# State sums of a selective scan: transposing accumulation replaced by identity matmuls with h as the moving operand, backward direction in reversed time

## The chip, the cores and the metric

The kernel runs on one core of a Trainium2 chip. The metric is the device time of one execution in microseconds (us), as the median of several runs. A profile is of one profiled execution; its span runs from the first to the last instruction of the program. The engines are TensorE (PE in the profile; PEld is its weight load, which can run beside a matmul), VectorE (DVE), ScalarE (ACT), GpSimd (POOL) and SyncE (SP), whose queue issues the DMAs.

## The reference

Four layers work on x of shape (16, 256, 256): an adapter of low rank, a bidirectional selective state-space layer with an MLP, and two attention blocks with MLPs. All is float32. The change lies in the state-space layer. For each of the two directions it computes this, the backward one on a flipped sequence whose result is flipped back:

```
def _ssm(h, in_w, xproj_w, dt_bias, A_log, Dskip, out_w):
    xz = h @ in_w
    xs, z = jnp.split(xz, 2, axis=-1)
    xs = jax.nn.silu(xs)
    proj = xs @ xproj_w
    dt = jax.nn.softplus(proj[..., :D_INNER] + dt_bias)
    Bm = proj[..., D_INNER:D_INNER + D_STATE]
    Cm = proj[..., D_INNER + D_STATE:]
    A = -jnp.exp(A_log)
    def step(hst, ins):
        dt_t, B_t, C_t, x_t = ins
        dA = jnp.exp(dt_t[:, :, None] * A)
        hst = hst * dA + (dt_t * x_t)[:, :, None] * B_t[:, None, :]
        y_t = jnp.einsum('bds,bs->bd', hst, C_t)
        return (hst, y_t)
    ...
    y = jnp.swapaxes(ys, 0, 1) + xs * Dskip
    return y * jax.nn.silu(z) @ out_w
...
h_fwd = _ssm(h, fwd_...)
h_bwd = jnp.flip(_ssm(jnp.flip(h, 1), bwd_...), 1)
x = x + gate * (h_fwd + h_bwd)
```

There are 512 inner channels, 64 states and 256 positions for each of 16 sequences in the batch.

## The kernel before

**Units and steps.** A unit is one sequence b in one direction d (0 forward, 1 backward), so there are 32 units. Each unit is worked off state by state: step k = (u, s) handles state s of unit u, for all 512 channels and 256 positions at once. There are 2048 steps. A tile of a step holds 128 partitions (channels within a block) x 4 blocks x 256 positions.

**One step.** `drive` (L931, POOL) makes h = dt·x·B for the state; the B rows come from DRAM, spread over the partitions by a DMA. `decay` (L946, ACT) makes exp(dt·A) into one of three PSUM tiles, two channel blocks at a time. `scan` (L974, DVE) runs the recurrence over time in place in h, in two instructions of 128x512. Then h is multiplied by the state's C row: in five of eight steps on DVE (L977), with the row spread over the partitions by two transposes on TensorE (`spread`, L961) into a double-buffered PSUM tile `cs`; in the other three steps on POOL (L981), with the row fetched by a DMA. `add_up` (L992, PE) adds h to the unit's sum `y` in PSUM. It does so by eight 128x128 transposes with accumulation: a block of h is the stationary operand, the identity is the moving one, and `y` has time on the partitions and channels along the free dimension. In the first step of a unit the skip term x·D is added in the same way.

**Backward units.** Their tensors stand in forward time. `decay` reads dt through a reversed view (`when`), takes the channel blocks in reversed order, and the scan works on a reversed view of h.

**End of a unit.** Two steps after the last scan of a unit, the sum leaves PSUM: ACT copies it (`yt`, L1165), eight transposes bring it back to channels on the partitions (`py`, L1172), and DVE multiplies it by the gate silu(z) out of PSUM (`yg`, L1173, two of 128x512). `back` then applies the output weights (`po`, L473) and adds the result to x (L480).

**Beside the scan** run the preparation of a later unit (`front`: input and dt projections, copies at L398, Silu, B and C rows) and the remaining layers of the previous sequence (`rest`: MLP, two attentions, two more MLPs), cut into small pieces by generators. One piece of `front` and one or two of `rest` are taken per step.

**What sets the order.** The kernel is written in Tile: the source gives dependencies and a program order in which `drive` is 4 steps ahead of the scan (`AHEAD`) and `add_up` 2 steps behind (`BEHIND`). A planner with its own instruction costs then fixes one order for each engine at build time, and each engine runs its list strictly in that order. The products on POOL are pinned to the program order. A step's h is one of eleven tiles (`NH`), which the skip term shares; `y` is a single PSUM tile of two banks, the three decays take three banks, `cs` one, and the work beside has two.

Of the kernel before, what the change touches and what calls it, by code (L numbers as in the profile page):

```python
# [15 lines left out]
P = 128  # L16
# [38 lines left out]
def kernel(ctx: ExitStack, tc: tile.TileContext, a: dict, out: bass.AP):  # L55
# [317 lines left out]
    def front(u):  # L373
# [15 lines left out]
        for m in range(0, 2 * IC, 2):  # L389
            px = halves(bank1("pxz"))  # L390
            for j in range(2):
                for c in range(DC):
                    nc.tensor.matmul(  # L393
                        px[:, j], w_in[:, c, (m + j) * P : (m + j + 1) * P], hT[:, c],
                        start=(c == 0), stop=(c == DC - 1),
                    )
                yield
            nc.scalar.copy(xz[:, m : m + 2], px)  # L398
        nc.scalar.activation(xz, xz, AF.Silu)
        exp_table()  # L400
        yield
# [63 lines left out]
    def back(u, yg):  # L465
# [12 lines left out]
        for m in range(DC):  # L478
            xb = xs[b][:, m]
            nc.vector.scalar_tensor_tensor(  # L480
                xb, po[:, m], m_mamba[:, 4 + m, b : b + 1], xb, ALU.mult, ALU.add
            )
        if d == 1:
            waiting.append(rest(b))
# [450 lines left out]
    def decay(k):  # L935
        u, s = steps[k]
        d = units[u][1]

        when = slice(1, T) if d == 0 else slice(T - 2, None, -1)
        made[k] = []  # L940
        for i in range(2):
            dc = decays[turn[0] % ND]
            turn[0] += 1
            for j in range(2):
                c = 2 * i + (j if d == 0 else 1 - j)
                nc.scalar.activation(  # L946
                    dc[:, j, 1:T], st[u][3][:, c, when], AF.Exp, scale=a_neg[d][:, c, s : s + 1]
                )
            made[k].append(dc)

# [13 lines left out]

    def scan(k):
        u, s = steps[k]
        d = units[u][1]
        h = hs[k]
        for i, dc in enumerate(made.pop(k)):
            hv = h[:, 2 * i : 2 * i + 2].rearrange("p c t -> p (c t)")  # L970
            dv = dc.rearrange("p c t -> p (c t)")
            if d == 1:
                hv = hv[:, ::-1]
            nc.vector.tensor_tensor_scan(hv, dv, hv, 0.0, ALU.mult, ALU.add)  # L974
        if k in nth:
            c = cs[:, nth[k] % 2]
# [7 lines left out]
    def add_up(k):  # L984
        u, s = steps[k]
        if s == 0:
            ys[u] = ps_y.tile([P, NT, DI], F32, name="y")

        for n, h in enumerate(([skips.pop(u)] if s == 0 else []) + [hs.pop(k)]):
            for t in range(NT):  # L990
                for c in range(IC):
                    nc.tensor.matmul(  # L992
                        ys[u][:, t, c * P : (c + 1) * P], h[:, c, t * P : (t + 1) * P], ident,
                        start=(s == 0 and n == 0 and c == 0),
                        stop=(s == NS - 1 and c == IC - 1), is_transpose=True,
                        skip_group_check=True,
                    )

# [144 lines left out]
    for k in range(len(steps) + BEHIND):  # L1145
# [13 lines left out]
        if k >= BEHIND:  # L1159
            u, s = steps[k - BEHIND]  # L1160
            if s == NS - 1:
                b, d = units[u]
                yt = s1.tile([P, NT, DI], F32, name="yt", tag="uu")
                for t in range(NT):
                    nc.scalar.copy(yt[:, t], ys[u][:, t])  # L1165
                yg = s1.tile([P, IC, T], F32, name="yg", tag="pr")
                for i in range(2):
                    py = halves(bank1("py"))
                    for j in range(2):
                        c = 2 * i + j  # L1170
                        for t in range(NT):
                            nc.tensor.transpose(py[:, j, t * P : (t + 1) * P], yt[:, t, c * P : (c + 1) * P], ident)  # L1172
                    nc.vector.tensor_tensor(  # L1173
                        yg[:, 2 * i : 2 * i + 2], py, st[u][0][:, IC + 2 * i : IC + 2 * i + 2], ALU.mult
                    )
                pend = beside((u, yg), u + 2)
        step(pend)
        for _ in range(2 if k % 2 else 1):
# [36 lines left out]
```

## Time and profile before

| | us |
|---|---|
| median of 3 runs | 7622.63 (7620.03 to 7626.16) |
| span of the profiled execution | 7616.3 |
| DVE busy | 6860.6 |
| POOL busy | 6843.8 |
| PE busy | 6249.2 |
| ACT busy | 5431.2 |
| sums over the states (L992), PE busy | 2385.3 |

The profiled execution's own time is not listed apart from its span; the median lies 6.3 us above the span. Busy time of an engine is the time covered by its instructions. A matmul's record includes the time in which it passes through the array, so records that follow closely overlap: their mean duration is longer than the pace at which they follow each other, and the pace is read from the length of an unbroken run. In a group's line the part after the bar gives the busy time, the mean in ns, and the idle time of the engine just before these instructions, with what ended most of it. In a table by stretch each engine has its busy time and, in brackets, its number of instructions.

### The profile page before, as it was taken

How to read it: one execution, taken by the hardware profiler on the slowest of the kernel's cores; microseconds unless marked ns; L12 is line 12 of the kernel's file. 1: busy time of each engine (PE TensorE's matmuls, PEld its weight loads, DVE VectorE, ACT ScalarE, POOL GpSimd, SP SyncE). 2: the span in 40 equal slices, each digit the busy share in tenths (PEclk: the TensorE clock that was granted, in tenths of full speed). 3: DMA queues.
4: the chain of work that ended last, by engine and by line, in shares of the span. 5: the costliest groups of instructions: out<-in, count | busy, mean ns of one | idle time of the engine just before them, and what ended most of it. 6: DMA issues, size and time to landing. Idle time of an engine off the chain costs nothing.

```text
span 7616.3 us, 100847 instructions
## 1 busy us (share of the span) xinstructions
PE 6249.2 (82%) x35471; PEld 4952.4 (65%) x35471; DVE 6860.6 (90%) x6887; ACT 5431.2 (71%) x12141; POOL 6843.8 (90%) x2959
## 2 busy tenths in 40 slices
PE   7568888888888888888888888888888888888778
PEld 4456676666667666676666666666666766666655
DVE  3988999999999999999999999999999999999982
ACT  4567777777777777777777777777777777777753
POOL 3999999999999999999999999999999999999960
PEclk8679999999999999999999999999999999999999
DMA  4112232222322222232222223222232222322221
GB/s 166 54 65 92 89 102 76 87 92 88 103 85 93 80 91 95 92 103 73 88 92 91 100 86 98 78 92 93 87 106 79 94 84 89 101 91 89 73 68 49
DMA packets 331644, 675.90 MB, mean 89 GB/s; under 512 B 24724, under 2 KB 204032, under 8 KB 326784
## 3 DMA queue, kind: packets, MB, share of 16 engines
q1 hardware_dynamic: 331136, 669.44, 26.7%
q8 instruction: 280, 4.59, 0.2%
q14 instruction: 228, 1.87, 0.1%
HBM read 650.22 MB, written 10.75 MB: 87 GB/s over the span
## 4 chain that ended last, share of the span: by engine, by line
DVE 47%; POOL 15%; issue 14%; ACT 12%; PE 10%; DVEq 0%; POOLq 0%; ACTq 0%
DVE h L974 34%; POOL h L931 8%; DVE h L977 8%; ACT decay L946 5%; POOL h L981 5%; PE y L992 3%; DVE maxima L682 1%; ACT L155 1%; PE dense L500 1%; PE down L511 1%; PE bank L108 1%; PE po L605 1%; POOL uu L452 1%; POOL dt L458 1%; POOL dtx L461 1%
## 5 line engine op out<-in xcount | busy, mean ns | idle before, releaser
L974 DVE TENSOR_TENSOR_SCAN h<-decay,h 128x512 f32<-128x512 f32 x4096 | 4748.8, 1213 | 283.1 <-ACT decay L946 196.6
L931 POOL TENSOR_TENSOR h<-dtx,bb 128x1024 f32<-128x1024 f32 x2048 | 4793.5, 2367 | 129.2 <-PE y L992 128.4
L992 PE MATMUL y<-ident,h 128*128 128x128 f32 x16384 | 2385.3, 292 | 693.0 <-POOL h L981 639.1
L992 PEld LDWEIGHTS y<-ident,h 128*128 128x128 f32 x16384 | 2054.6, 151 | 1047.6 <-POOL h L981 733.1
L946 ACT ACTIVATE decay<-dt,a_neg_bwd 128x255 f32<-128x255 f32 x4096 | 1816.8, 471 | 759.9 <-DVE h L974 718.3
L946 ACT ACTIVATE decay<-dt,a_neg_fwd 128x255 f32<-128x255 f32 x4096 | 1824.6, 474 | 613.0 <-DVE h L974 571.6
L981 POOL TENSOR_TENSOR h<-h,cb 128x1024 f32<-128x1024 f32 x768 | 1813.2, 2361 | 289.8 <-DVE h L974 275.1
L977 DVE TENSOR_TENSOR h<-h,cs 128x1024 f32<-128x1024 f32 x1280 | 1533.5, 1215 | 66.2 <-PE cs L961 56.6
L961 PE MATMUL cs<-ident,cT 128*128 128x128 f32 x2560 | 521.6, 294 | 131.8 <-DVE h L977 130.3
L961 PEld LDWEIGHTS cs<-ident,cT 128*128 128x128 f32 x2560 | 331.4, 147 | 216.0 <-DVE h L977 192.0
L572 PE MATMUL sc<-k,q 64*128 64x256 f32 x960 | 293.4, 429 | 16.7 <-ACT ex L581 16.0
L393 PE MATMUL pxz<-hTm,w_in 128*128 128x256 f32 x1024 | 267.6, 388 | 15.9 <-DVE maxima L682 12.1
L679 PE MATMUL sc<-kd,qk 128*128 128x512 f32 x490 | 251.4, 614 | 33.5 <-DVE maxima L682 20.8
L700 PE MATMUL scT<-qk,kd 128*128 128x256 f32 x984 | 251.1, 386 | 28.7 <-DVE qk L691 23.2
L581 ACT ACTIVATE ex<-sc,nmax 128x256 f32<-128x256 f32 x480 | 222.7, 468 | 71.2 <-DVE nmax L577 68.5
L423 PE MATMUL pdt<-xz,w_dt 128*128 128x256 f32 x1024 | 247.3, 385 | 0.0
L572 PEld LDWEIGHTS sc<-k,q 64*128 64x128 f32 x960 | 172.6, 200 | 105.3 <-issue 34.2
L393 PEld LDWEIGHTS pxz<-hTm,w_in 128*128 128x128 f32 x1024 | 181.4, 194 | 53.1 <-DVE maxima L682 15.5
L700 PEld LDWEIGHTS scT<-qk,kd 128*128 128x128 f32 x984 | 175.5, 190 | 60.7 <-ACT pr L429 25.0
L577 DVE TENSOR_REDUCE nmax<-sc 128x2 f32<-128x512 f32 x240 | 163.9, 683 | 49.5 <-PE sc L572 48.8
L423 PEld LDWEIGHTS pdt<-xz,w_dt 128*128 128x128 f32 x1024 | 190.7, 194 | 22.2
L595 ACT COPY exT<-pt 128x512 f32<-128x512 f32 x240 | 140.0, 583 | 86.2 <-PE pt L591 84.0
(350 smaller groups left out, 7571.4 us busy)
## 6 DMA issues: line engine op xcount, KB each, us to landing
bb<-bd SPq DMA_DIRECT2D x512, 512.0 KB
cb<-bd SPq DMA_DIRECT2D x256, 384.0 KB
l2w<-in_L_cond_W_dram SPq DMA_DIRECT2D x32, 1024.0 KB
l3w<-in_L_cond_W_dram SPq DMA_DIRECT2D x32, 1024.0 KB
l1w<-in_L_cond_mlp_w_dram SPq DMA_DIRECT2D x48, 512.0 KB
w_in<-in_L_cond_fwd_in_w_dram SPq DMA_DIRECT2D x16, 1024.0 KB
w_dt<-_L_cond_fwd_xproj_w_dram SPq DMA_DIRECT2D x16, 1024.0 KB
w_in<-in_L_cond_bwd_in_w_dram SPq DMA_DIRECT2D x16, 1024.0 KB
```

Source lines behind the costliest of these rows:

```text
L393: nc.tensor.matmul(px[:, j], w_in[:, c, (m + j) * P : (m + j + 1) * P], hT[:, c], start=(c == 0), stop=(c == DC - 1),)
L423: nc.tensor.matmul(pp[:, j], w_dt[:, c, (m + j) * P : (m + j + 1) * P], xz[:, c], start=(c == 0), stop=(c == IC - 1),)
L572: nc.tensor.matmul(sc[:, t], q[base : base + 64, ch, t * P : (t + 1) * P], k[base : base + 64, ch], start=True, stop=True,)
L679: nc.tensor.matmul(sc, q[:, g, t * P : (t + 1) * P], kd[g % 2][:, 2 * i : 2 * i + 2], start=True, stop=True)
L700: nc.tensor.matmul(sc[:, kt], kd[g % 2][:, j, kt * P : (kt + 1) * P], q[:, g], start=True, stop=True)
L931: nc.gpsimd.tensor_tensor(h, st[u][4], bb.unsqueeze(1).to_broadcast([P, IC, T]), ALU.mult)
L946: nc.scalar.activation(dc[:, j, 1:T], st[u][3][:, c, when], AF.Exp, scale=a_neg[d][:, c, s : s + 1])
L961: nc.tensor.transpose(cs[:, i % 2, t * P : (t + 1) * P], st[u][1][:, t, s : s + 1].to_broadcast([P, P]), ident)
L974: nc.vector.tensor_tensor_scan(hv, dv, hv, 0.0, ALU.mult, ALU.add)
L977: nc.vector.tensor_tensor(h, h, c.unsqueeze(1).to_broadcast([P, IC, T]), ALU.mult)
L981: nc.gpsimd.tensor_tensor(h, h, c.unsqueeze(1).to_broadcast([P, IC, T]), ALU.mult)
L992: nc.tensor.matmul(ys[u][:, t, c * P : (c + 1) * P], h[:, c, t * P : (t + 1) * P], ident, start=(s == 0 and n == 0 and c == 0), stop=(s == ...
```

## The change

The sum of a unit is kept with channels on the partitions. A step is added by two matmuls, each with the identity as the stationary operand and 512 columns of h (two channel blocks x 256 positions) as the moving one. At the end of a unit one DVE instruction multiplies the sum in PSUM by the gate; the copies, the transposes and the second multiply are gone. The backward direction is turned round where it enters and where it leaves: the copy of the input projection out of PSUM reads it in reversed time, and the output is added to x through a reversed view. Between the two all is in running order, so decay and scan have no reversed views.

```diff
-            nc.scalar.copy(xz[:, m : m + 2], px)
+            nc.scalar.copy(xz[:, m : m + 2], px[:, :, ::-1] if d else px)
...
-                xb, po[:, m], m_mamba[:, 4 + m, b : b + 1], xb, ALU.mult, ALU.add
+                xb, po[:, m, ::-1] if d else po[:, m], m_mamba[:, 4 + m, b : b + 1], xb, ALU.mult, ALU.add
...
-        when = slice(1, T) if d == 0 else slice(T - 2, None, -1)
...
-                c = 2 * i + (j if d == 0 else 1 - j)
+                c = 2 * i + j
                 nc.scalar.activation(
-                    dc[:, j, 1:T], st[u][3][:, c, when], AF.Exp, scale=a_neg[d][:, c, s : s + 1]
+                    dc[:, j, 1:T], st[u][3][:, c, 1:T], AF.Exp, scale=a_neg[d][:, c, s : s + 1]
...
-            if d == 1:
-                hv = hv[:, ::-1]
             nc.vector.tensor_tensor_scan(hv, dv, hv, 0.0, ALU.mult, ALU.add)
...
-            ys[u] = ps_y.tile([P, NT, DI], F32, name="y")
+            ys[u] = ps_y.tile([P, IC, T], F32, name="y")
...
-            for t in range(NT):
-                for c in range(IC):
-                    nc.tensor.matmul(
-                        ys[u][:, t, c * P : (c + 1) * P], h[:, c, t * P : (t + 1) * P], ident,
-                        start=(s == 0 and n == 0 and c == 0),
-                        stop=(s == NS - 1 and c == IC - 1), is_transpose=True,
-                        skip_group_check=True,
-                    )
+            for i in range(0, IC, 2):
+                nc.tensor.matmul(
+                    ys[u][:, i : i + 2], ident, h[:, i : i + 2],
+                    start=(s == 0 and n == 0), stop=(s == NS - 1),
+                )
...
-                yt = s1.tile([P, NT, DI], F32, name="yt", tag="uu")
-                for t in range(NT):
-                    nc.scalar.copy(yt[:, t], ys[u][:, t])
                 yg = s1.tile([P, IC, T], F32, name="yg", tag="pr")
-                for i in range(2):
-                    py = halves(bank1("py"))
-                    for j in range(2):
-                        c = 2 * i + j
-                        for t in range(NT):
-                            nc.tensor.transpose(py[:, j, t * P : (t + 1) * P], yt[:, t, c * P : (c + 1) * P], ident)
-                    nc.vector.tensor_tensor(
-                        yg[:, 2 * i : 2 * i + 2], py, st[u][0][:, IC + 2 * i : IC + 2 * i + 2], ALU.mult
-                    )
+                nc.vector.tensor_tensor(yg, ys[u], st[u][0][:, IC:], ALU.mult)
                 pend = beside((u, yg), u + 2)
```

More of the change, by code (lines that the diff above doesn't have):

```diff
@@ L966, in scan @@
         u, s = steps[k]
-        d = units[u][1]
         h = hs[k]
```

## The prediction

> **What bounds the kernel now.** I read the page first, for the busy times and the costliest groups; then the timeline of TensorE, for what one step's sums cost now and will cost; then the table of busy times by stretch, for where TensorE has room.
>
> ```profile
> PE 6249.2 (82%) x35471; PEld 4952.4 (65%) x35471; DVE 6860.6 (90%) x6887; ACT 5431.2 (71%) x12141; POOL 6843.8 (90%) x2959
> L974 DVE TENSOR_TENSOR_SCAN h<-decay,h 128x512 f32<-128x512 f32 x4096 | 4748.8, 1213 | 283.1 <-ACT decay L946 196.6
> L931 POOL TENSOR_TENSOR h<-dtx,bb 128x1024 f32<-128x1024 f32 x2048 | 4793.5, 2367 | 129.2 <-PE y L992 128.4
> L992 PE MATMUL y<-ident,h 128*128 128x128 f32 x16384 | 2385.3, 292 | 693.0 <-POOL h L981 639.1
> L977 DVE TENSOR_TENSOR h<-h,cs 128x1024 f32<-128x1024 f32 x1280 | 1533.5, 1215 | 66.2 <-PE cs L961 56.6
> ```
>
> Two engines share the lead: DVE (scans and 1280 of the multiplies by C) and POOL (products with B, and the other 768 multiplies), 90% each. TensorE looks close behind, but its 693 us of idle time ahead of the sums are waits for POOL's multiplies: it is ahead of its inputs. The kernel has 2048 steps (32 units of 64 states), and one takes about 3.54 us.
>
> The timeline of TensorE (start, length, then the instruction) holds one step's sums, and elsewhere two ordinary fp32 matmuls of the very shape that the change introduces:
>
> ```profile
> 3001.01 1.04 PE L992 MATMUL y<-ident,h 128*128 128x128 f32 x8
> ...
> 3857.76 1.88 PE L773 MATMUL pv<-wv,hT 128*128 128x512 f32 x4
> ```
>
> Eight transposes take 1.04 us: the last one's own 0.273, and 0.109 for each before it. Two 128x512 matmuls stand as four records (each fp32 matmul is recorded twice) and take 1.88 us: 0.592 for the last, 0.429 for each before it. In a full queue a step's sums thus occupy TensorE for 8 x 0.109 = 0.87 us now and 4 x 0.429 = 1.72 us after.
>
> Next the 128 steps of one batch in the middle, cut at the end of every sixteenth scanned state, so that each row is 16 steps. First all engines, then the sums of L992 alone:
>
> ```profile
> core 0: us, PE busy (x) PEld busy (x) DVE busy (x) ACT busy (x) POOL busy (x), PEclk, DMA share, GB/s
> 3764.90:3815.90 51.00, 40.76 (x236) 34.69 (x234) 49.47 (x49) 37.35 (x79) 48.41 (x21) 0.97 0.30 93
> 3815.90:3872.00 56.10, 51.59 (x258) 41.11 (x259) 48.51 (x46) 48.94 (x104) 46.53 (x21) 0.94 0.47 158
> 3872.00:3938.10 66.10, 54.51 (x353) 42.25 (x351) 59.24 (x59) 46.56 (x131) 66.10 (x30) 0.92 0.16 52
> 3938.10:3993.40 55.30, 41.10 (x217) 31.01 (x216) 51.74 (x52) 36.63 (x90) 52.47 (x23) 0.81 0.19 58
> 3993.40:4053.30 59.90, 51.39 (x304) 41.95 (x302) 55.53 (x60) 43.72 (x90) 51.22 (x22) 1.00 0.33 109
> 4053.30:4106.70 53.40, 47.33 (x238) 34.26 (x238) 52.99 (x58) 42.09 (x92) 51.21 (x22) 1.00 0.29 95
> 4106.70:4162.30 55.60, 50.80 (x340) 39.17 (x339) 55.32 (x56) 41.60 (x91) 54.28 (x24) 1.00 0.23 75
> 4162.30:4221.60 59.30, 45.85 (x272) 39.31 (x265) 52.99 (x55) 40.86 (x89) 57.40 (x25) 0.91 0.27 86
> ...
> 3764.90:3815.90 51.00, 15.51 (x108) 13.41 (x106) 0.97 0.30 93
> 3815.90:3872.00 56.10, 15.24 (x104) 13.37 (x104) 0.94 0.47 158
> 3872.00:3938.10 66.10, 25.73 (x183) 21.91 (x183) 0.92 0.16 52
> 3938.10:3993.40 55.30, 19.66 (x125) 16.77 (x123) 0.81 0.19 58
> 3993.40:4053.30 59.90, 17.67 (x134) 15.29 (x134) 1.00 0.33 109
> 4053.30:4106.70 53.40, 13.27 (x99) 11.47 (x98) 1.00 0.29 95
> 4106.70:4162.30 55.60, 20.11 (x152) 17.52 (x152) 1.00 0.23 75
> 4162.30:4221.60 59.30, 20.75 (x142) 18.00 (x143) 0.91 0.27 86
> ```
>
> The reader is to see that DVE and POOL take turns at 97 to 100%, and that TensorE's load moves with the dense layers and attentions of the batch before, which run beside the scan. The second row holds only 104 transposes, 13 steps' worth, for 16 scanned states: there the sums already fall behind, and the third row makes up for it (183).
>
> **The change part by part.**
>
> *Sums, the term that decides.* The sums of a step grow by 1.72 - 0.87 = 0.85 us, over 2048 steps 1,740 us of TensorE work, in 7,240 us of loop. TensorE's other work in a row is its busy time less L992's: 25.3, 36.4, 28.8, 21.4, 33.7, 34.1, 30.7 and 25.1 us. With 16 x 1.72 = 27.5 us for the sums, and 0.7 more in rows one and five (below), a row needs 53.5, 63.9, 56.3, 48.9, 61.9, 61.6, 58.2 and 52.6 us of TensorE. Five of the eight are longer than now: by 2.5, 7.8, 2.0, 8.2 and 2.6 us, 23.1 in a batch, 370 us over 16 batches. The whole batch needs 457 us of TensorE where it takes 456.7 now: even smoothed perfectly, nothing is left over.
>
> Backlog that can be carried from a heavy row into a light one takes some of this back. It sits in the eleven h tiles, and the C rows in PSUM are double-buffered: L961 can spread the next but one only after a multiply has let go. The built program shows that the planner uses this up beforehand: on DVE a multiply by C now stands 1.4 scanned states behind its own scan on the mean, after the change 5.9. So six of eleven tiles wait to be summed by plan. Bounds: nothing, to two steps (7 us) for each of the two heavy stretches of a batch, which are 0 to 224 us. I take 2 us a stretch, near nothing because of those six tiles: -64 us.
>
> The opposite bound is that TensorE is not busy all the time where it is the limit, because its queue is in order and matmuls beside wait for ScalarE: no row above shows it over 92% (51.59 of 56.10). That is priced among the rivals.
>
> *A page weighed against these rows.* The Trainium skill, "TensorE: Matmul & The Clock Gate", Back-to-back issue gap, gives pairs of weight load and matmul some 81 ns at 128 columns and 131 ns at 512; by that a step would go from 8 x 81 = 648 to 2 x 131 = 262 ns, no row would be over, and the time would be some 7,600 us. The same page, Terms, says that the transpose mode is four times faster for FP32, which speaks against giving it up. Per column the two timeline rows give 0.85 ns transposed and 2 x 0.429 / 512 = 1.68 ns as a matmul: half the page's ratio, but far from its issue gap. I go by the rows.
>
> *Sums with weights that stay.* The loads of h (L992's PEld) become loads of ident. They run beside the matmuls in both forms (the 1.88 us row has its loads inside); nothing.
>
> *End of a unit.* Gone are ScalarE's two copies (L1165, 64 x 582 ns), eight transposes (L1172, 1.04 us as above) and two multiplies of 690 ns (L1173); in their place stands one 128x1024 multiply from PSUM, nearest row L977 with 1.215 us. DVE gains 1.38 - 1.215 = 0.165 us, 32 times: -5 us. ScalarE's 37 us lie in rows one and five, where it is busy 73%; it comes to the fore only through the decays that DVE waits for (196.6 us in all), so 0 to -37, and I take 0 because DVE is busy 97 and 93% there. TensorE loses the 1.04 us, and the sum of the skip term, which is not among the sixteen of a row, takes 1.72: the 0.7 more in rows one and five.
>
> *The new wait.* DVE's multiply waits for the last sums, and all scans behind it wait with it. In the planned order the last multiply before it stands three scans (3.6 us) ahead, and the two sums between take 3.4 + 0.16: hidden. If TensorE is a sum late, 32 x 1.9 = 61 us; at most 0 to 61, taken as 0, since the units change in a row with room. TensorE's first sums of the next unit wait for that multiply, 1.2 us, as they did for ScalarE's copies, 1.16: nothing.
>
> *Reversed time.* The scan and the decays lose their reversed views. The decays' two groups have 474 (forward) and 471 ns: nothing. For DVE I compared the scans in 215 us of the forward unit (138.6 us for 121) and of the backward one (139.7 us): 1.1 us a unit, at most 19 us over 16 units; I take -10. Reversed reads arrive in 64 copies of 579 ns (L398) and 32 multiplies of 488 ns (L480); no row shows a reversed read from PSUM. From 0 to twice as long: 37 us of ScalarE and 16 of DVE at most; the decays, where reversing cost nothing, are the nearest row, so 0.
>
> *Order.* POOL's list is unchanged. On SP's queue a few weight loads change places with loads of B and C rows; POOL shows no wait for these now. Nothing, unless a weight load waits long for its buffer; then a share of the upper bound.
>
> Sum: +370 - 64 - 5 - 10 = +291 us on the span of 7616.3: 7,907. The median of the runs shown, 7622.63, is 6.3 us above the span; with as much around it, 7,914 us.
>
> **The rivals.**
>
> *TensorE blocked in its own queue.* If it gets no further than 95% in any row and nothing is carried, the rows need 56.3, 67.2, 59.2, 51.5, 65.2, 64.8, 61.3 and 55.4 us; five are over, by 5.3, 11.1, 5.3, 11.4 and 5.7, 38.8 a batch, 621 in all: about 8,230 us. For it: ScalarE's and DVE's places in order are fixed, and a late matmul holds up the decays. Against it: in a backlog there is always a sum to run.
>
> *The longer lag pays: faster.* The multiplies' 5.9 states of lag give each TensorE result longer before it is needed. DVE is busy 425.8 of 456.7 us in the batch (sum of its column); its 30.9 idle us, 494 over 16 batches, are what could go. A third of it is 165: 7,460 us. It takes that TensorE's other work shrinks in a full queue: eight 256-column matmuls last 1.89 us alone (0.379 + 7 x 0.216) and 1.73 in a stream, 9% less, so 236 becomes some 215 us, and 437 of TensorE would fit. It decides if the backlog can be carried across some 64 states; eleven tiles speak against that.
>
> *Nothing shows.* The backlog is absorbed: two steps are carried in each stretch, 370 - 224, and the heavy rows' other work, 160 us a batch, shrinks by 6% in a full queue (9 us a batch, 146 in all): 7,620 us. It takes two favourable bounds at once.
>
> **How the numbers follow.** TensorE becomes the limit in the heavy rows: 0.66, 7,914 us, itself between 7,750 (two steps carried in each stretch) and 8,050 (nothing carried, and the 61 us at the unit ends). Blocked in its queue: 0.20. Faster: 0.10. No change within 0.2% (about what a measurement here can tell): 0.04. The range reaches from 7,640, just over the case of no change, to 8,240, the blocked case; outside remain the faster case and the worst of the blocked one. Slower 0.86, same 0.04, faster 0.10.
>
> **What would show it.** TensorE's busy share rises from 82% to over 92%, while DVE and POOL fall to some 86%. The group of the sums has 8192 records and over 3,400 us. POOL's wait for the sums (128.4 us) and DVE's for the C rows (56.6) grow at least twofold. The chain that ended last names TensorE for a third or more, where it was 10%. The rows with dense layers grow by 2 to 8 us, the others hardly. The forecast is wrong if the record of a 128x512 sum takes much less than 0.43 us in a stream, or if the heavy rows stay as they are: then the tiles carried more than I allow.

## The result and the profile after

The changed kernel takes 8833.39 us (median; 8832.55 to 8839.97) where the kernel before takes 7624.4: a ratio of 1.158, 95% interval 1.157 to 1.160. Forecast were 7,914 us with a range of 7,640 to 8,240. The direction was right; the loss is 1,209 us, four times the 291 forecast. The profiled execution has a span of 8838.2 us.

The page of the kernel after: busy times, the chain's shares by engine, and the groups that answer to those shown of before.

```profile
PE 7730.6 (87%) x26895; PEld 4442.1 (50%) x26895; DVE 6919.1 (78%) x6855; ACT 5490.7 (62%) x12077; POOL 6842.7 (77%) x2959
...
POOL 39%; issue 24%; PE 17%; DVE 15%; ACT 4%; DMA 0%; POOLq 0%; SPq 0%; DVEq 0%; ACTq 0%
...
L931 POOL TENSOR_TENSOR h<-dtx,bb 128x1024 f32<-128x1024 f32 x2048 | 4806.7, 2364 | 1603.9 <-PE y L987 1566.2
L970 DVE TENSOR_TENSOR_SCAN h<-decay,h 128x512 f32<-128x512 f32 x4096 | 4772.7, 1208 | 1349.8 <-POOL h L931 1259.0
L987 PE MATMUL y<-h,ident 128*128 128x512 f32 x8192 | 3997.6, 613 | 78.6 <-POOL h L977 78.6
...
L973 DVE TENSOR_TENSOR h<-h,cs 128x1024 f32<-128x1024 f32 x1280 | 1508.7, 1206 | 150.8 <-PE cs L960 150.0
```

DVE and POOL do the same work in nearly the same time as before (DVE 58 us more, POOL 1 less); they only wait. POOL's wait for the sums went from 128 to 1,566 us, and DVE's wait for POOL's products (81 us before, in its list of waits) to 1,259. TensorE itself hardly waits for multiplies any more (79 us, before 639). Its busy time grew by 1,481 us (6249.2 to 7730.6) while the span grew by 1,222: its idle time fell only from 1,367 to 1,108 us. TensorE is now the fullest engine, at 87%: 1,367 us of room were there, and 259 of it were used.

The chain of work that ended last puts 17% on TensorE and 39% on POOL, though TensorE is the one that is late. The chain follows a product of POOL back to the sum that let go its tile, and from there on through the engines; the wait turns up where the tiles are missing.

The same eight rows of a middle batch as in the prediction, cut at the same scanned states; the columns are the same:

```profile
core 0: us, PE busy (x) PEld busy (x) DVE busy (x) ACT busy (x) POOL busy (x), PEclk, DMA share, GB/s
4315.50:4380.10 64.60, 52.79 (x176) 30.75 (x174) 52.99 (x54) 38.03 (x80) 51.01 (x23) 0.95 0.23 75
4380.10:4465.50 85.40, 79.45 (x292) 51.86 (x290) 52.37 (x51) 56.81 (x109) 52.49 (x23) 1.00 0.32 107
4465.50:4530.60 65.10, 58.85 (x197) 29.81 (x198) 54.84 (x55) 43.22 (x117) 63.51 (x28) 0.90 0.19 65
4530.60:4582.40 51.80, 46.47 (x178) 23.07 (x174) 51.07 (x49) 39.17 (x103) 49.58 (x23) 1.00 0.19 61
4582.40:4641.80 59.40, 49.84 (x177) 30.78 (x176) 53.63 (x55) 34.01 (x79) 49.23 (x22) 1.00 0.20 65
4641.80:4716.90 75.10, 69.74 (x234) 40.65 (x234) 57.16 (x63) 47.14 (x96) 50.24 (x22) 1.00 0.24 83
4716.90:4786.70 69.80, 64.35 (x236) 37.01 (x236) 55.89 (x58) 46.30 (x91) 58.35 (x26) 0.98 0.24 78
4786.70:4851.40 64.70, 53.32 (x184) 29.62 (x183) 51.72 (x50) 37.51 (x85) 53.22 (x23) 0.95 0.19 61
sum 535.90, PE 474.80 PEld 273.54 DVE 429.68 ACT 342.19 POOL 427.62; mean PE 59.35 PEld 34.19 DVE 53.71 ACT 42.77 POOL 53.45
```

and of these, the sums alone:

```profile
sum 535.90, PE 252.85 PEld 97.26; mean PE 31.61 PEld 12.16
```

Against before the rows change by +13.6, +29.3, -1.0, -3.5, -0.5, +21.7, +14.2 and +5.4 us: 79.2 in the batch, times 16 some 1,270 us. Rows three to five run as before; TensorE has 21.5, 15.7 and 22.5 us beside the sums there (its busy time less that of the sums). Little work beside the sums does not spare a row by itself, though: the first has 18.8 us and grew by 13.6. In the second row TensorE is busy 93% and DVE and POOL 61%. TensorE's idle time in the eight rows is 61.1 us; in the rows before it was 73.4 (456.7 less 383.3 busy).

What the idle time looks like, in the timeline just ahead of the first row (start, length, instruction; in brackets the idle time before it and what ended it):

```profile
4299.94 1.02 PE L987 MATMUL y<-h,ident 128*128 128x512 f32 x2
...
4302.45 1.22 DVE L970 TENSOR_TENSOR_SCAN h<-decay,h 128x512 f32<-128x512 f32 x1 [2.27 <-POOL h L931]
4303.59 0.66 DVE L103 TENSOR_TENSOR hT<-x,bank 128x512 f32<-128x512 f32 x1
...
4305.30 1.22 PE L108 MATMUL bank<-sq,onesm 128*128 128x256 f32 x4 [4.33 <-ACT sq L105]
4308.02 2.67 PE L987 MATMUL y<-h,ident 128*128 128x512 f32 x4
...
4311.61 3.62 PE L500 MATMUL dense<-hT,l3w 128*128 128x256 f32 x16
...
4316.15 3.62 PE L500 MATMUL dense<-hT,l3w 128*128 128x256 f32 x16
...
4319.60 3.60 PE L987 MATMUL y<-h,ident 128*128 128x512 f32 x8
...
4321.56 2.36 POOL L931 TENSOR_TENSOR h<-dtx,bb 128x1024 f32<-128x1024 f32 x1 [8.43 <-PE y L987]
...
4323.96 2.34 DVE L970 TENSOR_TENSOR_SCAN h<-decay,h 128x512 f32<-128x512 f32 x2 [3.16 <-POOL h L931]
```

TensorE stands still for 4.33 us ahead of a normalization's matmul (L108), which waits for ScalarE's squares; these wait for DVE's hT (L103), which stands in DVE's order behind a scan, which waits for POOL's product. Meanwhile the sum of step 1012 (counted over the whole run), multiplied since 4283.78, stands behind that matmul and starts at 4308.02. Then step 1014, multiplied at 4307.63, stands behind 32 records of dense matmuls until 4319.60; its tile comes free at 4321.48, and POOL, which has waited 8.43 us for it, makes the next product. That is a ring: TensorE, POOL, DVE, and by the work beside back to TensorE. I matched each sum in the trace with its multiply. Of the 1,022 us that TensorE is idle between the first and the last sum, 697 are time in which the next sum has its h multiplied and TensorE waits for another matmul that stands ahead of it (before: 405 of 1,289); a multiplied h waits 11.9 us on the mean for its sum (before: 5.0). Of the 697 us, 179 end in the dense layers (L500), 116 in the normalizations (L108) and 57 in the C rows.

### The profile page after: what moved, and what is told of

Its sections match the earlier page's. It is cut to its first block, busy times and chain, and to the rows that moved or that the text cites. A ratio compares the mean times of both kernels' runs of the same rounds, so it can differ in the third digit from the quotient of the medians.

```text
span 8838.2 us, 83571 instructions
## 1 busy us (share of the span) xinstructions
PE 7730.6 (87%) x26895; PEld 4442.1 (50%) x26895; DVE 6919.1 (78%) x6855; ACT 5490.7 (62%) x12077; POOL 6842.7 (77%) x2959
## 4 chain that ended last, share of the span: by engine, by line
POOL 39%; issue 24%; PE 17%; DVE 15%; ACT 4%; DMA 0%; POOLq 0%; SPq 0%; DVEq 0%; ACTq 0%
POOL h L931 28%; DVE h L970 10%; POOL h L977 9%; PE y L987 7%; PE dense L500 3%; DVE h L973 2%; ACT decay L945 2%; PE down L511 1%; PE sc L679 1%; POOL dtx L461 1%; POOL uu L452 1%; POOL dt L455 1%; PE scT L700 1%; POOL dt L458 0%; PE pdt L423 0%
## 5 line engine op out<-in xcount | busy, mean ns | idle before, releaser
L987 PE MATMUL y<-h,ident 128*128 128x512 f32 x8192 | 3997.6, 613 | 78.6 <-POOL h L977 78.6
L945 ACT ACTIVATE decay<-dt,a_neg_bwd 128x255 f32<-128x255 f32 x4096 | 1855.7, 471 | 1535.6 <-DVE h L970 1460.1
L987 PEld LDWEIGHTS y<-h,ident 128*128 128x128 f32 x8192 | 1537.9, 197 | 1435.3 <-issue 1271.1
L973 DVE TENSOR_TENSOR h<-h,cs 128x1024 f32<-128x1024 f32 x1280 | 1508.7, 1206 | 150.8 <-PE cs L960 150.0
L960 PEld LDWEIGHTS cs<-ident,cT 128*128 128x128 f32 x2560 | 342.3, 139 | 901.3 <-issue 541.8
L960 PE MATMUL cs<-ident,cT 128*128 128x128 f32 x2560 | 498.8, 278 | 205.8 <-DVE h L973 203.2
L393 PE MATMUL pxz<-hTm,w_in 128*128 128x256 f32 x1024 | 270.3, 389 | 24.5 <-DVE maxima L682 21.5
L591 PE MATMUL pt<-ident,ex 128*128 128x128 f32 x960 | 166.0, 299 | 86.8 <-ACT q L609 51.1
L591 PEld LDWEIGHTS pt<-ident,ex 128*128 128x128 f32 x960 | 113.5, 149 | 182.6 <-ACT q L609 86.0
```

Of the source, the lines that this page charges most:

```text
L393: nc.tensor.matmul(px[:, j], w_in[:, c, (m + j) * P : (m + j + 1) * P], hT[:, c], start=(c == 0), stop=(c == DC - 1),)
L945: nc.scalar.activation(dc[:, j, 1:T], st[u][3][:, c, 1:T], AF.Exp, scale=a_neg[d][:, c, s : s + 1])
L960: nc.tensor.transpose(cs[:, i % 2, t * P : (t + 1) * P], st[u][1][:, t, s : s + 1].to_broadcast([P, P]), ident)
L973: nc.vector.tensor_tensor(h, h, c.unsqueeze(1).to_broadcast([P, IC, T]), ALU.mult)
L987: nc.tensor.matmul(ys[u][:, i : i + 2], ident, h[:, i : i + 2], start=(s == 0 and n == 0), stop=(s == NS - 1),)
```

## The experiments

Several causes could be behind a loss so much over the forecast. One is load (L): the longer sums, together with the work beside, are more than TensorE can hide. Another is order (O): the planner, which held scans and multiplies 1.4 states apart before and 5.9 after, built a worse order. A third is the queue (K): matmuls beside that wait for other engines block the sums behind them. (The first four expectations call the load W, whichever way it acts.) Or it is another part of the change: reversed time, or the form of the matmul and of the sum in PSUM. A time given without a ratio is a single one.

### Each part by itself

**Reversed time alone.** The kernel before with only this part of the change:

```diff
-            nc.scalar.copy(xz[:, m : m + 2], px)
+            nc.scalar.copy(xz[:, m : m + 2], px[:, :, ::-1] if d else px)
...
-            if d == 1:
-                hv = hv[:, ::-1]
```

> The kernel before with the reversed time alone: transposing sums, ScalarE's copies and the transposes back stay. Theory W (TensorE's load per step decides) and theory O (the planned order, with multiplies six states behind their scans, decides) both expect -20 to +5 us against before, 7,605 to 7,630, since neither load nor lag changes (mean lag 1.4 states, as before). A third theory, that reversed reads out of PSUM are dear, expects +20 us or more, with the copy of the input projection over 0.6 us in backward units.

Measured: 7620.35 us, a ratio of 0.9997 (0.9988 to 1.0006). It is worth nothing, between 9 us gained and 5 lost, and the reversed reads out of PSUM cost nothing that shows in the time (the copies of L398 take 562 to 587 ns, and 563 to 588 before). The loss is elsewhere.

**Sums of half and of three quarters of the positions.** The form of after, but from the second state on only 128 (or 192) of the 256 positions are summed, so that part of each sum is left out:

```diff
+                q = T if s == 0 else T // 2
                 nc.tensor.matmul(
-                    ys[u][:, i : i + 2], ident, h[:, i : i + 2],
+                    ys[u][:, i : i + 2, 0:q], ident, h[:, i : i + 2, 0:q],
```

> The changed kernel, but from the second state on the sums take 128 of the 256 positions (half of the sum is left out). A step's sums then occupy TensorE for 4 x 0.216 = 0.86 us, as much as the eight transposes did; the form of the matmul, the identity as stationary operand, the end of a unit and the reversed time stay as changed. The planner goes back to a mean lag of 1.3 states. W and O both expect 7,560 to 7,640. If another part of the change costs the 1,200 us, it stays over 8,000.

> The changed kernel with 192 of the 256 positions in the sums from the second state on (a quarter of the sum is left out): 4 x 0.322 = 1.29 us a step. L expects a knee: TensorE's need passes that of the other engines only where the dense layers run, 7,680 to 7,800. K expects a time about halfway between 7,673 (half of the columns) and 8,833 (all): 8,100 to 8,350.

**Transposes, twice.** The kernel before, with each h added twice by its transposes, so that the sums hold twice their value:

```diff
+            for r in range(2):
                 for t in range(NT):
```

> The kernel before, with each h added twice by the eight transposes (the sum over the states is counted twice), so that a step's sums occupy TensorE for 16 x 0.109 = 1.74 us as in the changed kernel, but with h as stationary operand, time-major, and with nothing else of the change. L and K both expect 8,600 to 8,950. If the form of the sums costs something by itself (the identity as stationary operand, 512 columns written to PSUM by one instruction), it stays under 8,300.

Measured (half the positions with a ratio of 1.0066, 1.0053 to 1.0080; three quarters and twice one time each), with the price of a step's sums from the prediction's rows, scaled:

| kernel | sums per step, us | time, us | TensorE busy | POOL's wait for sums, us |
|---|---|---|---|---|
| before | 0.87 | 7,624 | 82% | 128 |
| half the positions | 0.86 | 7,673 | 82% | 128 |
| three quarters | 1.29 | 8,133 | 86% | 768 |
| after | 1.72 | 8,833 | 87% | 1,566 |
| transposes twice | 1.74 | 9,039 | 87% | 1,714 |

The page of the last:

```profile
PE 7893.3 (87%) x52111; PEld 6732.3 (75%) x52111; DVE 6930.3 (77%) x6887; ACT 5562.1 (62%) x12141; POOL 6868.9 (76%) x2959
...
L931 POOL TENSOR_TENSOR h<-dtx,bb 128x1024 f32<-128x1024 f32 x2048 | 4820.1, 2367 | 1783.6 <-PE y L993 1713.7
```

With the old price the new form costs 49 us; with the new price the old form costs as much as the change and 200 us more (a single time, over what either theory expected). So neither the identity as weights, nor the layout in PSUM, nor the end of a unit makes the loss, but the TensorE time of the sums, with the order that the planner builds for it: in the built order the multiplies stand 1.3, 4.6, 5.9 and 6.1 states behind their scans, from half to twice. And there is no knee, with little below some price of a sum and all of it above (the theory L in that form falls): the first 0.43 us a step (881 us of TensorE) cost 460 us, the second 700.

### Without the work beside

Both kernels with the later layers of each sequence left out (MLP, both attentions, two MLPs), so that only the preparation of units remains beside the scan:

```diff
-        hT = yield from norm3(b, m_mlp, 0)
...
-        yield from feed_forward(
-            b, "l3w1", "l3w2", hT, "L3_cond_b1", 3
-        )
```

> The kernel before with everything behind the state-space layer left out (its MLP and both attention layers with their MLPs; the x after the state-space layer is stored). TensorE's other work falls from 3,527 to 1,073 us. VectorE and GpSimd keep the whole scan. All theories expect GpSimd as the limit: 2048 x 3.25 + 128 x 2.37 + 160 us before and behind the loop = 7,120; 7,050 to 7,250.

> The changed kernel with the same layers left out. TensorE needs at most 1.72 + 1.27 = 2.99 us a step in any stretch of eight, less than VectorE and GpSimd. If the cost of the change is TensorE's sums together with the layers that run beside (theories L and K), it equals the ninth experiment within 50 us. If the longer sum costs by itself in the ring of one step (product, scan, multiply, sum, and the h tile back to the product), it is over 200 us slower than the ninth.

Measured: 7067.35 and 6968.72 us, one time each. The busy times on the page, with the sums of before, then those with the sums of after:

```profile
PE 4337.0 (61%) x23151; PEld 3798.6 (54%) x23151; DVE 6216.1 (88%) x5607; ACT 4317.5 (61%) x9213; POOL 6819.6 (97%) x2959
```

```profile
PE 5389.0 (77%) x14575; PEld 2625.7 (38%) x14575; DVE 6187.1 (89%) x5575; ACT 4241.8 (61%) x9149; POOL 6805.4 (98%) x2959
```

By itself, then, the longer sum does no harm: with 77% of TensorE taken, POOL still gets to 98%, and the change is 99 us faster. How much of the 99 us is the change's own is not shown: the granted clock was 0.76 in the one execution and 0.90 in the other. The longer sum becomes a loss only with the later layers beside it; they load DVE and ScalarE too, but the runs above tie the loss to TensorE's time for the sums.

### Is it the order?

**Every multiply right behind its scan.** On DVE, scans and multiplies are held to the program order (no lag), first with the long sums (from after), then with the cheap ones (from before):

```diff
-            nc.vector.tensor_tensor_scan(hv, dv, hv, 0.0, ALU.mult, ALU.add)
+            tc.keep_in_program_order(nc.vector.tensor_tensor_scan(hv, dv, hv, 0.0, ALU.mult, ALU.add))
...
-            nc.vector.tensor_tensor(h, h, c.unsqueeze(1).to_broadcast([P, IC, T]), ALU.mult)
+            tc.keep_in_program_order(
+                nc.vector.tensor_tensor(h, h, c.unsqueeze(1).to_broadcast([P, IC, T]), ALU.mult)
+            )
```

> The changed kernel with VectorE's scans and multiplies pinned to the program order, so that each multiply by C stands directly behind its own scan (mean lag 0.0 states, where the planner put 5.9). TensorE's work is the same. W expects 8,700 to 8,900. O expects most of the 1,200 us back: 7,850 to 8,100, with POOL's wait for the sums under 500 us (1,566 in the changed kernel).

> The kernel before with the multiplies pinned directly behind their scans, as in the third experiment, with the cheap transposing sums (mean lag 0.02 states). If the planned order is worth a few per cent by itself whatever the sums cost, 7,700 to 7,900, as with the sums in one pass (7,819, lag 0.5). If the 7,819 came from float32r or from the end of a unit, 7,600 to 7,650.

Measured: 8785.92 us with the long sums, 1.1525 (1.1509 to 1.1541), and 8421.84 with the cheap ones. The page with the long sums:

```profile
PE 7717.6 (88%) x26895; PEld 4361.2 (50%) x26895; DVE 6998.4 (80%) x6855; ACT 5539.4 (63%) x12077; POOL 6832.9 (78%) x2959
...
L931 POOL TENSOR_TENSOR h<-dtx,bb 128x1024 f32<-128x1024 f32 x2048 | 4776.5, 2359 | 0.1
...
L979 POOL TENSOR_TENSOR h<-h,cb 128x1024 f32<-128x1024 f32 x768 | 1807.3, 2353 | 1597.4 <-DVE h L970 1343.3
```

and two groups with the cheap ones:

```profile
L931 POOL TENSOR_TENSOR h<-dtx,bb 128x1024 f32<-128x1024 f32 x2048 | 4786.9, 2366 | 0.1
...
L983 POOL TENSOR_TENSOR h<-h,cb 128x1024 f32<-128x1024 f32 x768 | 1809.7, 2356 | 1227.9 <-DVE h L974 1030.9
```

Taking the lag away gains 47 us of 1,209, so no lag is no remedy (what O expected, 7,850 to 8,100 us, falls). That doesn't clear the lag, nor does it measure the load: the cheap sums lose 798 us in this list. With the long sums POOL no longer waits for a single sum, but for DVE's scans, 1,343 us; of these, 1,031 are there with the cheap sums too, so most of that wait belongs to the list and not to the sums. Nor is it the queue as in the kernel after: of TensorE's 979 us of idle time between the first and the last sum, only 165 have the next sum ready behind another matmul, where it was 697 of 1,022. The same time thus comes about in two ways.

**A lag of four states, and of one, with the cheap sums.** The kernel before, the DVE multiplies held four states behind in the program and the sums as much later; for one state `LATE` is 1 and `BEHIND` 3:

```diff
+    def late_multiply(k):
+        if k in nth:
+            c = cs[:, nth[k] % 2]
+            tc.keep_in_program_order(
+                nc.vector.tensor_tensor(hs[k], hs[k], c.unsqueeze(1).to_broadcast([P, IC, T]), ALU.mult)
+            )
...
+    LATE = 4
...
-    AHEAD, BEHIND = 4, 2
+    AHEAD, BEHIND = 4, 6
```

> The kernel before with its cheap transposing sums, but each multiply by C on VectorE pinned four states behind its own scan, and the sums taken six steps behind instead of two (mean lag 4.5 states, where it was 1.4). W expects 7,600 to 7,750, since TensorE's work is unchanged. O expects over 8,200, with POOL waiting over 800 us for the sums (128 before).

> The kernel before with each multiply on VectorE pinned one state behind its own scan and the sums three steps behind instead of two (mean lag 2.2 states). TensorE's work is unchanged. If a little slack between scan, C row and multiply is what the order lacks, VectorE's waits for C rows (57 us) and for decays (197) shrink: 7,450 to 7,600. If the planner's own order is already near the best, 7,620 to 7,750.

Measured: 7916.43 us, 1.0384 (1.0370 to 1.0398), with four states, and 7607.28 us, 0.9971 (0.9959 to 0.9982), with one. The last beats both kernels by a little. In the order that was built, multiplies stand 4.5 and 2.2 states behind their scans. Four states of lag cost 292 us though the sums are the same; tiles are taken for longer, and POOL's wait for sums goes from 128 to 631 us. One state (2.2 as built) costs nothing.

**The order of before, written down.** Scans and multiplies of both kernels are held to the lags that the planner gave the kernel before, state by state (a table `LAG` of 128 numbers that `late_multiply` goes by, with the scans held too; sums and C rows follow the multiplies in the program):

```diff
+        while late and k >= late[0] + LAG[late[0] % 128]:
+            late_multiply(late[0])
```

> Control for the next run: the kernel before with VectorE's scans and multiplies pinned to the order that the planner had given them (a table of lags, 1.8 states on the mean, up to 7 where the dense layers run), and each sum taken once its multiply is issued. The planner is free in all else. If order is carried by the scans and multiplies, 7,600 to 7,750. If pinning harms by itself, because matmuls beside and the rest of VectorE's list then fall elsewhere, it is over 7,900, and the next run is read against it.

> The changed kernel with the same table of lags (mean 1.9 states where its planner put 5.9). TensorE's work as changed. If TensorE's load makes the 1,209 us with any order, 8,700 to 9,000. If the planner's answer to the load (multiplies six states late) makes up most of them, 7,950 to 8,250.

Measured: 8665.17 us with the cheap sums and 9245.71 with the long ones. The first number is the lesson: the same sums with much the same lags as before (1.8 states on the mean, where it was 1.4), yet 1,041 us slower. That the work beside now has to find its place around a fixed list is my guess at the cause, and not shown. Holding an order on DVE is no neutral act here, and the pair says only that with this list the longer sums cost 581 us.

**The one harmless order, with the long sums.** The kernel after with `LATE = 1` and `BEHIND = 3` as above, and with 3 and 5:

> The kernel after with each DVE multiply by C held one state behind its scan and the sums three steps behind, the order that took the kernel before to 7,607 us. It holds the one order known to be harmless and changes only the price of a sum. If the longer sums as a load set the time, whatever the order, the time stays within 2% of the 8,833 us of the kernel after: 8,650 to 9,000, with TensorE at 86 to 89% and POOL's wait for the sums over 1,000 us. If a good part of the loss is the order that the planner answers with (5.9 states of lag), the time falls to the 7,972 us that the cheap sums in this order and the 364 us of the pair at no lag give, or at least under 8,400.

> The same with three states of lag and the sums five steps behind. If the load sets the time, the lag hardly matters: within 2% of the run at one state. If lag is what lets a late sum through, it is faster than at one state by 100 us or more; if held tiles are what hurts, slower by 100 us or more.

Measured: 9320.35 us, 1.2223 (1.2203 to 1.2244), and 9225.87 us. Neither theory had the first. The page of the first:

```profile
PE 7989.2 (86%) x26895; PEld 4554.7 (49%) x26895; DVE 6936.9 (74%) x6855; ACT 5512.6 (59%) x12077; POOL 6846.0 (73%) x2959
...
L931 POOL TENSOR_TENSOR h<-dtx,bb 128x1024 f32<-128x1024 f32 x2048 | 4800.1, 2356 | 2083.8 <-PE y L992 1907.5
L970 DVE TENSOR_TENSOR_SCAN h<-decay,h 128x512 f32<-128x512 f32 x4096 | 4774.9, 1207 | 1741.0 <-POOL h L931 1617.8
```

The order was not what I meant to hold: only the multiplies are held, and the planner again sent the scans ahead, 6.1 states on the mean (6.2 with three). So this is no clean test of load against order, and the pair, with nearly the same lag as built, says nothing on the lag. It does show the ring again, in its strongest form: of 1,250 us of TensorE's idle time between the first and the last sum, 949 have the next sum ready behind another matmul. And the planner's own answer, 8,833 us, is better than this one.

### Does it help to put the sums first, or to shorten them?

**Sums ahead of the rest.** The kernel with no lag and long sums, with a high priority for the sums in the planner:

```diff
+                with tc.high_priority():
                     nc.tensor.matmul(
                         ys[u][:, i : i + 2], ident, h[:, i : i + 2],
```

> The changed kernel with the multiplies pinned behind their scans as in the third experiment (8,786 us), and with a higher priority in the planner for the sums, so that they stand ahead of the matmuls that run beside. TensorE's work is the same, but in the planned order its other work between two sums is spread more evenly (at most 3.1 us a step in a stretch of eight steps, and 2.0 where it was 0.95 behind the first heavy stretch). L expects 8,650 to 8,850. K expects 8,000 to 8,450, with TensorE over 90% busy.

Measured: 10843.4 us (one time), the largest miss of all expectations. Two groups of the page:

```profile
L979 POOL TENSOR_TENSOR h<-h,cb 128x1024 f32<-128x1024 f32 x768 | 1802.4, 2347 | 3657.9 <-DVE h L970 2760.1
L974 DVE TENSOR_TENSOR h<-h,cs 128x1024 f32<-128x1024 f32 x1280 | 1552.7, 1217 | 961.6 <-PE cs L960 928.4
```

Sums put first stand in the queue ahead of the C rows (L960) and of the attention's scores (DVE's `nmax`, L577, waits 574 us for these), and DVE, waiting for them, holds up its scans. A matmul that waits blocks whatever stands behind it, a sum no less than the others. TensorE's idle time rose to 2,306 us, 1,913 of it ahead of sums (L990), mostly for multiplies that were not done. So turning the two round (K's remedy) doesn't help on this list. It was not tried on the kernel after, where the sums do stand behind other work: the list with no lag had only 165 us of that kind.

**Sums in one pass.** The kernel after with h and the identity as float32r, a number format in which the trace has one record for each of these matmuls where fp32 has two ("one pass"); all that writes h writes it in that format. The matmul's part of the edit:

```diff
-                    ys[u][:, i : i + 2], ident, h[:, i : i + 2],
+                    ys[u][:, i : i + 2], ident_r, h[:, i : i + 2].bitcast(mybir.dt.float32r),
```

and the same with the multiplies one and two states late:

> The changed kernel with h written in float32r by all that writes it, and the identity too, so that a 128x512 sum needs a single pass (h and its products are rounded to that format). Expected of a sum: one record, about 0.216 us in a stream, 0.43 us a step where the transposes took 0.87 and the fp32 matmuls 1.72. Theory L (TensorE is full) and theory K (TensorE is blocked in its own queue, behind matmuls that wait for ScalarE or VectorE) both expect 7,540 to 7,640: the cost of the change is gone, and what is left of it is the shorter end of a unit.

> The sums in one pass of float32r (fifth experiment, 7,819 us, mean lag 0.5), with each multiply on VectorE pinned one state behind its own scan and the sums three steps behind (mean lag 1.2). If the fifth run lost only through its order, as the eleventh and twelfth suggest, then the gain of the shorter unit end (99 us between the ninth and tenth) shows: 7,480 to 7,620. If float32r costs by itself, 7,750 or more.

> The same with two states of lag (mean 2.2, as in the twelfth experiment, 7,607 us). If lag is what the fifth run lacked: 7,480 to 7,620, below the fifteenth if the optimum lies where the planner put it for the transposes with one state more (2.2).

Measured: 7818.63 us, 1.0262 (1.0248 to 1.0276); 7615.07 us, 0.9989 (0.9979 to 0.9999); 7655.35 us, 1.0043 (1.0028 to 1.0058). The page of the first:

```profile
PE 5883.5 (75%) x22735; PEld 3977.4 (51%) x22735; DVE 6865.2 (88%) x6856; ACT 5406.3 (69%) x12077; POOL 6845.6 (88%) x2959
...
L989 PE MATMUL y<-h,ident_r 128*128 128x512 f32 x4096 | 1849.0, 537 | 1216.6 <-POOL h L979 1080.7
L979 POOL TENSOR_TENSOR h<-h,cb 128x1024 fp32r<-128x1024 f32 x768 | 1811.0, 2358 | 593.1 <-DVE h L972 517.0
```

The same form at a quarter of the price (0.43 us a step, worked out below, where it was 1.72) gives back 1,015 of the 1,209 us. What is left of the loss goes with the order: with one state of lag it is gone. But sums cheaper than those of before gain nothing either: at 7,607 to 7,615 us the kernel stands on DVE and POOL, which are busy 90% each.

### What is settled and what is open

The cause is TensorE's time for the sums in company of the later layers: with the same form and cheaper sums the loss goes but for 49 us (half) or 194 (one pass), with the old form and dearer sums it comes (twice), and without the later layers the change is a gain. Open is how the 1,209 us split between the load and the order that the planner builds for it. With the order held in both kernels the longer sums cost 364 us (no lag) and 581 us (table), but on kernels that holding had made 10 to 14% slower, so that TensorE had more room (1,782 us idle with no lag and cheap sums, 1,367 before); and order alone moved the cheap-sum kernel from 7,607 to 8,665 us. No order tried brings the two-pass sums under 8,786 us. Open, too, is by which way of the ring the time is lost in general: in the kernel after sums stand behind waiting matmuls, with no lag they mostly don't, and the time is the same. Eleven of the eighteen runs lie outside every range that was expected of them.

## Why the prediction was wrong in size, point by point

**Step "Sums, the term that decides": the price was right, the room was not.** A 128x512 record follows the last at 0.429 us, there are 8192 of them, and rows three to five hardly changed, where 0, 0 and 2.0 us were forecast. The row sum failed in three ways; for the batch shown it gave 479.8 us (456.7 + 23.1) of which TensorE busy 457, and it took 535.9 with 474.8 busy.

- *The bound set aside.* "The opposite bound is that TensorE is not busy all the time where it is the limit": that was the step that failed. The row sum let TensorE run without a gap in every heavy row, which leaves 22.8 us idle in the batch; it was 61.1. That is 38 us of the miss of 56. Even the rival priced it at 95%, and in the heavy rows alone. Over the span it gets to 87%, 93% in its heaviest row, and it is 82% in the first and last row of the batch, which nevertheless grew by 13.6 and 5.4 us. The argument against, "in a backlog there is always a sum to run", holds for 697 of the 1,022 idle us and does not help: the sum is there and stands in the queue behind a matmul that waits. The rows before had shown it: that DVE and POOL take turns at 97 to 100% does not hold in the second row, where DVE has 86% and POOL 83%; TensorE, at 92% the fullest engine there, still left 4.5 us idle.
- *The rows' own price.* I took TensorE's other work as its busy time less the group of the sums. That group's 147.9 us in the eight rows contain the time through the array, 1.16 us a step; what I put in its place, 1.72 us a step, was a pace without it. Measured by the same column the sums after take 252.85 us (525 records), 1.95 a step over the whole run. TensorE's busy time grew by 91.5 us in the batch where I had 74: the other 18 of the 56.
- *Where the rows are cut.* The cut was by scanned states, and the prediction itself saw that the second row held only 13 steps' worth of sums. Counted in TensorE's own order from sum to sum, TensorE is busy 4.6 us a step over steps 8 to 24 after the change, and less 1.72 for the sums the work beside is 2.9. The cut by scans had shown 36.4 us beside in the second row; there were 49.0 (79.45 less 30.41). The neighbours gave it up (18.8 and 21.5 where 25.3 and 28.8 were expected), so it moves the loss between rows (row six grew by 21.7 where 8.2 was forecast, row five not at all) more than it makes one.

Times 16, the miss of a batch is 898 us, where the span is 931 over the 7,907 forecast; the 79 us taken off for other terms did not show, and the batch shown lost 45 us more (over sixteen) than the whole run did.

**"I take 2 us a stretch" for the backlog carried:** nothing of the 64 us shows. The tiles in which scanned states wait for their multiply, and multiplied ones for their sum, are the ones POOL waits for.

**The rival of the blocked queue** had the mechanism that the kernel after shows, and was priced at 8,230 us: too little by 600, for the reason just given. A sum on whole-engine times comes nearer than the rows: 6249.2 busy and 1,740 more are 7,989 us; at the 90% that DVE and POOL, the fullest engines of the profile before, reach, that is 8,877 us, 0.5% over what came. Two errors cancel in it, and that is luck: TensorE was busy 7,731 us and not 7,989, and 87% and not 90%. The same rule gives 7,899 us for three quarters of the positions (6249.2 and 2048 x 0.42; measured 8,133) and 8,923 for the doubled transposes (6249.2 and 2048 x 0.87; measured 9,039): short by 3 and 1%, and found after the fact. It knows nothing of the order, which took the same sums from 8,786 to 10,843 us.

**"The longer lag pays: faster"** fell. Four states of lag with cheap sums cost 3.8%; one state gained 0.3%.

**End of a unit** (-5 us) was not measured by itself. **The new wait** was taken as nothing. DVE's wait for the last sums is 11 us in all, so the bound of 61 was not reached. TensorE's waits for `yg`, taken as 1.2 us each, are 105 us (31 of them, 3.4 each), where 35 us stood before ahead of the transposes that waited for ScalarE's copies. The 70 us more are small beside the ring. **Reversed time:** -10 us was taken; measured alone, -2 with an interval of -9 to +5. That reversed reads from PSUM cost nothing held within that interval.

**What would show it:** 8192 records and 3,998 us, right. POOL's wait grew twelvefold and DVE's for C rows from 57 to 150 us, right (at least twofold). TensorE over 92%: wrong (87%). DVE and POOL at some 86%: wrong (78 and 77%). The chain with a third on TensorE: wrong, 17%; it names POOL.

**The page weighed.** The Trainium skill, "TensorE: Matmul & The Clock Gate", Back-to-back issue gap, has 131 ns for a pair of weight load and matmul at 512 columns. These fp32 sums follow each other at 0.858 us (two records of 0.429), so going by the rows was right. Its section Terms has the transpose mode four times faster for FP32; here it is two times (0.85 against 1.68 ns a column), and giving it up is what doubled the price.

## What to carry to other kernels

When work is added to an engine that is already 82% busy and shares a ring of buffers with two others at 90%, do not count on its idle time: the extra load used a fifth of it here (259 of 1,367 us), and in the eight runs with dearer sums beside the later layers TensorE got no fuller than 88% over the span (86 to 88% in seven, 79% where the sums were put first). A first estimate from this is the new busy time over a fill of 86 to 88%; at 87% the three busy times worked out above give times 0.5 to 4% too long. It is one kernel's number, and the order can add to it. And where a wait shows up (POOL's, in chain and waits) is where buffers run out, not which engine is late: the cheap test is to scale the suspected engine's work up and down, as with half, three quarters and twice the sums.

## What the runs showed of the hardware

- A 128x512 sum in float32r is one record, where fp32 has two, and two of them last 0.71 us when they follow each other. From the timeline of the one-pass kernel:

```profile
3026.01 0.71 PE L989 MATMUL y<-h,ident_r 128*128 128x512 f32 x2
```

  Less the 0.497 us of one record by itself (the median) that is a pace of some 0.21 us, half that of an fp32 record: a step costs 0.43 us, half of the transposes.
- The granted clock went with TensorE's busy share: 0.93 before (82%) and 0.96 after (87%), 0.85 with the sums in one pass (75%), but 0.76 without the later layers (61%) and 0.90 without them and with the long sums (77%). At 0.76 the 16384 transposes were busy for 3,029 us, 351 ns a record, where they took 2,385 and 292 before, on a TensorE that had 39% to spare.
- The order on one engine is worth nearly as much as the change (1,058 us between the best and the worst): with the same cheap sums, holding DVE's list in one way or another gave 7,607, 7,916, 8,422 and 8,665 us.
